# The first layer of a graph network moved into the cells of the later layers, edges sorted by pairs of node blocks, and the second layer set apart

## The chip, the cores and the metric

The kernel runs on one core of a Trainium2 chip. The metric is the device time of one execution in microseconds (us). Before the change it is 16670.39 us, the median of 10 runs that lie between 16644.18 and 16690.65.

A core has several engines that work side by side, each with a queue of its own in program order: PE (matrix multiplication), DVE (elementwise vector work), ACT (activations and copies), POOL (a second, slower vector engine, which here issues nearly all indirect transfers) and SP (which issues most plain transfers). Transfers run on 16 DMA engines. PE accumulates in PSUM, a memory of eight banks.

## The reference

A graph has N = 12500 nodes with 48 features and E = 400000 edges, sorted by their destination `dst`; `src` is random. Four graph layers follow each other, each with `x = layernorm(x + layer(x))`:

```python
# layer 0, edge attributes of width 32
h = relu(concat([x[dst], x[src], edge_attr_32]) @ W1 + b1)        # hidden 128
out = segment_sum(h @ W2 + b2, dst)
# layer 1: ci, cj from the degrees of src and dst
out = relu(where(in_deg > 0, segment_sum((x * ci)[src], dst) * cj, x) @ W.T + b)
# layer 2: row = src, col = dst
out = relu((segment_sum(norm * x[dst], src)) @ W.T + b)
# layer 3, edge attributes of width 40, per-edge gate
gate = silu(edge_attr_40 @ W1.T + b1) @ W2.T + b2 + sum(emb[z[src]] * (emb[z[dst]] @ adaptW.T))
msg = gate * x[dst] * (cutoff(distance) * node_mult[dst])
out = layernorm(x + segment_sum(msg, src) / clip(segment_sum(node_mult[dst], src)))
```

Layer 0 therefore needs, for each edge, a value of its source and of its destination, and sums by destination; layers 2 and 3 take from the destination and sum by source.

## The kernel before

Nodes lie in NB = 98 blocks of 128 and, two by two, in NP = 49 pairs. A *cell* is a pair of destination blocks (256 nodes) together with one source block (128 nodes); it has 128 slots for its edges. With one edge per lane, the cells of one destination pair make a matrix of 128 slots by 98 source blocks. Once an edge sits in a slot, its source features are picked out by a matrix multiplication with a one-hot matrix (its source block is known), and sums go through another one-hot matrix. No transfer per edge is needed then. All is in `by_cells` (line 55), and runs in stages that follow each other:

- **Histogram** (L291 to L311): the degree of every source. A hardware loop of 25 rounds takes 125 chunks of 128 edges each. For each chunk DVE makes two one-hot matrices, `c_ol` (L307) of the low seven bits and `c_oh` (L309) of the high bits, and PE multiplies them into PSUM.
- **Flat copies and tables** (L314 to L443): `dst`, `src` and the cutoff factor are turned by PE transposes and written flat to memory; `starts` holds where each block's edges begin. `qtab` holds, per source node, `x @ W1b` (128 values) and its embedding (32); `ptab` holds, per destination node, `x @ W1a + b1`, the adapted embedding and `node_mult` (161 values), split in three bfloat16 parts whose sum is the float32 value.
- **Layer 0** (L446 to L544): a hardware loop over the 98 destination blocks. A block's edges are read through a window of CW = 34 chunks of 128. DVE makes one one-hot matrix of the whole window, `c_wturned` (L482, 128 by 4352). For each chunk POOL gathers 128 rows of `qtab` with an indirect transfer (L260, called at L501), PE adds the edge attributes' part (L508) and the destination's part through the one-hot matrix and the three parts of `ptab` (L513), DVE adds the gathered rows (L529) and makes the products of the embeddings (L530), ACT applies relu (L532), and PE sums into the block by a float32 one-hot matrix `c_whot` (L522, L534). Per edge, the logit and `node_mult` go to `lmtab`.
- **Bias and layer norm** of layer 0, and the features of layer 1 in three parts.
- **Edges to cells, and layer 1** (L552 to L812), written out without a hardware loop. `to_cells` (L588) takes the 34 chunks of a block in steps of four: a one-hot matrix of the source block (L618), the gate's first layer on PE over the transposed attributes `c_sea` (L625), silu on ACT (L628), then per chunk PE's running counts `c_pp` (`tri`, L634), DVE's rank of the edge in its cell from them (L638), the gate's second layer on PE (L641), and `rest` (L642), which completes the counts and waits for the rank. ACT forms the record (L646). Every 12 chunks `scatter` (L657) works out where each edge goes, and POOL writes one record of 51 values per edge with an indirect transfer per chunk (L686). Layer 1 of an earlier pair (`layer1`, L735) is a Python generator; `advance` runs two of its steps after each four chunks, so its instructions stand between those of `to_cells` in the queues.
- **Middle of layer 1** (to L837): degree scaling, a 48 by 48 linear map, layer norm.
- **Layer 2** (L840 to L908): a hardware loop of 7 rounds of 14 source blocks; for each, the 49 pairs' features by one-hot matrices (`c_dhot` L869, L883), sums by `c_os` (L876).
- **Layer 3** (from L911): a hardware loop of 7 rounds of 7 pairs; per pair its records `c_rc` are read, features picked by `c_phot` (L962, L972), added up from three parts (L985), multiplied into the records (L988), and summed for each of the 98 source blocks by a float32 one-hot matrix (L980, L944) into the accumulator `c_acc` (L947).

`gather` (L259) and `one_hots` (L268, whose line stands for every caller in the profile: L270) are helpers. Within a stage, the order on each engine is settled by the compiler's scheduler from the written order and the buffers that come free. A flag, counted from broken assumptions (edges not sorted, a cell with over 128 edges, a window too small), chooses a slow general path at the end; on these inputs it isn't taken.

Of the kernel before, what the change touches and what calls it, by code (L numbers as in the profile page):

```python
# [54 lines left out]
def by_cells(ctx: ExitStack, tc: tile.TileContext, a: dict, out: bass.AP, flag):  # L55
# [17 lines left out]
    CW = -(-int(E / NB + 4.2 * (E / NB) ** 0.5) // P)  # L73
    W = CW * P
    UP = largest_divisor(NP, 7)
    UB = 2 * UP
# [4 lines left out]
    Q0 = HID + DG  # L81
    R = D + 3
    D3 = 3 * D
    CELLS = NB * SLOTS
    DUMP = NI * CELLS
    KP = -(-NB // 3)
    CP = 12
# [6 lines left out]
    src_f = dram.tile([E], I32, name="c_src_f")  # L94
    dst_f = dram.tile([E], I16, name="c_dst_f")
    cut_f = dram.tile([E], F32, name="c_cut_f")
    dst_rows = dram.tile([NCH, P], F32, name="c_dst_rows")
    first_f = dram.tile([P], I32, name="c_first_f")
    qtab = dram.tile([NB * P, Q0], F32, name="c_qtab")
    ptab = dram.tile([NB * P, 3 * T0], BF16, name="c_ptab")  # L100
    embtab = dram.tile([a["emb"].shape[0], 2 * DG], F32, name="c_embtab")
    lmtab = dram.tile([NB * P, 2 * CW], F32, name="c_lmtab")
    htab = dram.tile([NB * P, D], F32, name="c_htab")
    recs = [dram.tile([DUMP + 2 * NI * W, R], F32, name=f"c_rec{u}") for u in range(UP)]

    pair_d = dram.tile([NP, CELLS], BF16, name="c_pair_d")
    block_d = dram.tile([NB, NP * SLOTS], BF16, name="c_block_d")

# [11 lines left out]
    cols_f = const.tile([P, P], F32, name="c_cols_f")  # L120
    nc.vector.tensor_copy(cols_f, cols_i[:, :P])
    cols1_b = const.tile([P, 2 * P], BF16, name="c_cols1_b")
    nc.vector.tensor_scalar(cols1_b, cols_i, 1.0, None, op0=ALU.add)
    cols1_f = const.tile([P, P], F32, name="c_cols1_f")
    nc.vector.tensor_scalar(cols1_f, cols_i[:, :P], 1.0, None, op0=ALU.add)
# [9 lines left out]
    deg1 = const.tile([P, UB], F32, name="c_deg1")  # L135
# [5 lines left out]
    dump_i = const.tile([P, 2 * NI, CW], I32, name="c_dump_i")  # L141
    nc.gpsimd.iota(dump_i, pattern=[[W, 2 * NI], [1, CW]], base=DUMP, channel_multiplier=CW)
    dump_at = const.tile([P, 2 * NI, CW], F32, name="c_dump_at")
# [3 lines left out]
    block_i = const.tile([P, NB], I32, name="c_block_i")  # L147
    nc.gpsimd.iota(block_i, pattern=[[P, NB]], base=0, channel_multiplier=0)
    block_at = const.tile([P, NB], F32, name="c_block_at")
    nc.vector.tensor_copy(block_at, block_i)  # L150
# [28 lines left out]
    nc.sync.dma_start(w1c[0:DE, :], a["L0_W1"][2 * D : 2 * D + DE, :])  # L179
    w2 = load("w2", [HID, D], a["L0_W2"])  # L180
# [3 lines left out]
    g1T = load("g1T", [DR, D], a["L3_W1T"])  # L184
# [83 lines left out]
    def one_hots(o, codes, n, w):  # L268

        nc.vector.tensor_tensor(  # L270
            o[:, :n, :].rearrange("p j (a t) -> p j a t", t=2),
            cols1_b[:, :w].rearrange("p (o a t) -> p o a t", o=1, t=2).to_broadcast([P, n, w // 2, 2]),
            codes[:, :, None, :].to_broadcast([P, n, w // 2, 2]),
            op=ALU.is_equal,
        )

    def window_at(b):
        return nc.values_load(
            starts[0:1, ds(b, 1)] if not isinstance(b, int) else starts[0:1, b : b + 1],
            engines=(ET.SP,),  # L280
            min_val=0,
            max_val=E - W,
            skip_runtime_bounds_check_because="the smaller of two, and not negative",
        )

    def of_window(t, at):

        return t[ds(at, W)].rearrange("(p c) -> p c", c=CW)


    nc.vector.memset(degs["src"], 0.0)  # L291
    with tc.tile_pool(name="c_hk", bufs=2) as hk, tc.tile_pool(name="c_hoh", bufs=6) as hoh, tc.tile_pool(
        name="c_hps", bufs=1, space=PSUM
    ) as hps:
        with tc.For_i(0, NCH, CA) as i:
# [3 lines left out]
            for part, op, arg in (("hi", ALU.logical_shift_right, 7), ("lo", ALU.bitwise_and, 127)):  # L299
                v_i = hk.tile([P, CA], I32, name=f"c_{part}_i")  # L300
                nc.vector.tensor_scalar(v_i, ki, arg, None, op0=op)
                half[part] = hk.tile([P, CA], F32, name=f"c_{part}")
                nc.vector.tensor_copy(half[part], v_i)
            pd = hps.tile([P, NB], F32, name="c_pd")
            for c in range(CA):
                ol = hoh.tile([P, P], BF16, name="c_ol")
                nc.vector.tensor_scalar(ol, cols_b, half["lo"][:, c : c + 1], None, op0=ALU.is_equal)  # L307
                oh = hoh.tile([P, NB], BF16, name="c_oh")
                nc.vector.tensor_scalar(oh, cols_b[:, :NB], half["hi"][:, c : c + 1], None, op0=ALU.is_equal)  # L309
                nc.tensor.matmul(pd, ol, oh, start=(c == 0), stop=(c == CA - 1))  # L310
# [3 lines left out]
    with tc.tile_pool(name="c_fe", bufs=1) as fe, tc.tile_pool(name="c_few", bufs=3) as few, tc.tile_pool(  # L314
# [18 lines left out]
        for key in ("dst", "src", "cut"):  # L333
            kf = fold
            if key != "cut":
                ki = fe.tile([P, NCH], I32, name=f"c_fki_{key}")
                nc.sync.dma_start(ki, a[key + "T"])
                kf = fe.tile([P, NCH], F32, name=f"c_fkf_{key}")
                nc.vector.tensor_copy(kf, ki)
            for c in range(0, NCH, CT):  # L340
                pt = fep.tile([CT, P], F32, name="c_fpt")
                nc.tensor.transpose(pt, kf[:, c : c + CT], ident)
                flat, kind = {"src": (src_f, I32), "dst": (dst_f, I16), "cut": (cut_f, F32)}[key]
                t = few.tile([CT, P], kind, name=f"c_ft_{key}")
                (nc.vector.tensor_copy if key == "dst" else nc.scalar.copy)(t, pt)
                nc.sync.dma_start(flat.rearrange("(c p) -> c p", p=P)[c : c + CT, :], t)
                if key == "dst":
                    u = few.tile([CT, P], F32, name="c_ft_row")
                    nc.scalar.copy(u, pt)
                    nc.scalar.dma_start(dst_rows[c : c + CT, :], u)  # L350
# [17 lines left out]
        low = fe.tile([P, 1], F32, name="c_flow")  # L368
        nc.vector.tensor_scalar(low, first, float(E - W), None, op0=ALU.min)
# [183 lines left out]
    with tc.tile_pool(name="c_s1", bufs=1) as s1:  # L553
# [12 lines left out]
        with tc.tile_pool(name="c_s1r", bufs=2) as lr, tc.tile_pool(name="c_s1t", bufs=1) as lt, tc.tile_pool(  # L566
# [237 lines left out]
            for p in (NP - 2, NP - 1):  # L804
                if p < 0:
                    continue
# [881 lines left out]
```

## Time and profile before

The profiled execution's own time is 16669.57 us; its span from the first to the last instruction is 16667.8 us, so 1.8 us lie outside. The mean granted clock of PE is 0.739 of full speed. The page gives the busy shares of the span: PE 77%, PE's weight loads 60%, DVE 58%, POOL 42%, ACT 32%.

The stages can be told apart in the page's 40 slices and bounded in the timeline:

| stage | from to (us) | length (us) | per unit |
|---|---|---|---|
| histogram | 0 to 1104 | 1104 | 44.2 per round |
| copies and tables | 1104 to 1416 | 312 | |
| layer 0 | 1416 to 6135 | 4719 | 48.16 per block |
| bias, norm | 6135 to 6216 | 81 | |
| to cells, layer 1 | 6216 to 11844 | 5628 | 114.9 per pair |
| middle of layer 1 | 11844 to 12000 | 156 | |
| layer 2 | 12000 to 13188 | 1188 | 12.1 per block |
| its end | 13188 to 13344 | 156 | |
| layer 3 | 13344 to 16570 | 3226 | 65.8 per pair |
| end | 16570 to 16668 | 98 | |

How to read the views: *busy* is the time in which an engine had an instruction under way; instructions overlap on PE, so a mean duration there is longer than the distance from one start to the next. That distance, taken from the timeline, is what one instruction costs when many follow each other. The *granted clock* is a share of PE's full speed. A group of instructions has its line, engine, operation, output and inputs, count, busy time and mean, and then the idle time before them with what ended it.

### The profile page before, as it was taken

Reading aid. Unit: us, or ns where it says so; the run is one execution under the profiler, and the core shown is the slowest. Engines: PE = TensorE matmul, PEld = TensorE weight load, DVE = VectorE, ACT = ScalarE, POOL = GpSimd, SP = SyncE. Lnnn points to the kernel's source line nnn. Section 1 sums busy time; section 2 is a strip of 40 time slices with the busy share of each in tenths; the row PEclk is TensorE's granted clock in tenths of the full one; section 3 lists DMA queues with packets and bytes.
Section 4 is the critical chain, followed back from the end, with each engine's and each line's share of the span. In section 5 each row is a group of like instructions: output and inputs, shape, how many; then the busy total and the mean of one; then the engine's idle time right before and its main releaser. Section 6 shows DMA issues by size and latency. Waiting matters only on the chain. (4 is left out here: it accounts for less than half of the span.)

```text
span 16667.8 us, 263542 instructions
## 1 busy us (share of the span) xinstructions
PE 12760.9 (77%) x90916; PEld 9936.1 (60%) x90917; DVE 9585.4 (58%) x34506; ACT 5293.4 (32%) x11631; POOL 7078.5 (42%) x6776
## 2 busy tenths in 40 slices
PE   6655666666666559989988989988698788888886
PEld 2225555555555545555555555555587677777776
DVE  9974443443444443444444444444577688888888
ACT  0004444444444434444444444444366500000000
POOL 0006777777777755666566666666200000000000
PEclk9999888878878875666666666666699866666666
DMA  0025444444444432222222222222233222222222
GB/s 2 1 42 145 117 132 120 124 126 120 125 122 127 122 89 72 81 79 86 80 80 86 82 79 87 87 74 85 79 125 141 83 94 93 87 84 93 87 87 65
DMA packets 604921, 1537.81 MB, mean 92 GB/s; under 512 B 298614, under 2 KB 458790, under 8 KB 514518
## 3 DMA queue, kind: packets, MB, share of 16 engines
q1 hardware_dynamic: 280116, 1009.83, 18.9%
q0 software_dynamic: 269728, 363.67, 8.9%
q10 hardware_dynamic: 53778, 147.83, 2.3%
q8 instruction: 713, 11.68, 0.3%
q14 instruction: 586, 4.80, 0.1%
HBM read 1270.69 MB, written 250.08 MB: 91 GB/s over the span
## 5 line engine op out<-in xcount | busy, mean ns | idle before, releaser
L686 POOL DMA_INDIRECT c_rec<-c_srt,c_sat x3332 | 3393.6, 1018 | 2276.2 <-issue 1305.2
L260 POOL DMA_INDIRECT c_wq<-c_qtab,c_wix x3332 | 3581.9, 1075 | 1175.3 <-issue 953.4
L638 DVE CUSTOM_DVE_ANT_0 c_sjunk<-c_pp,c_soh 128x98 f32<-128x98 f32 x3332 | 857.3, 257 | 2255.6 <-PE c_pp L634 2246.9
L508 PE MATMUL c_wpl<-c_w1c,c_eat 128*128 128x128 f32 x6664 | 1177.3, 307 | 1176.6 <-ACT c_lm L531 971.2
L944 PE MATMUL c_pa<-c_rc,c_os 128*128 128x49 f32 x9604 | 1861.3, 347 | 252.1 <-DVE c_rc L988 251.5
L944 PEld LDWEIGHTS c_pa<-c_rc,c_os 128*128 128x128 f32 x9604 | 1718.1, 263 | 352.4 <-issue 167.3
L625 PE MATMUL c_sph<-c_sea,c_g1T 40*48 40x512 f32 (+1 forms) x1764 | 1778.4, 1097 | 21.5 <-ACT c_hid L628 21.5
L508 PEld LDWEIGHTS c_wpl<-c_w1c,c_eat 128*128 128x128 f32 x6664 | 979.2, 213 | 1200.1 <-ACT c_lm L531 989.8
L534 PE MATMUL c_wpa<-c_whot,c_wh 128*128 128x128 f32 x6664 | 1188.8, 329 | 638.8 <-ACT c_lm L531 606.4
L641 PE MATMUL c_spg<-c_g2x,c_hid 128*128 128x48 f32 x6664 | 1438.5, 372 | 141.0 <-ACT c_srt L646 137.8
L646 ACT ACTIVATE c_srt<-c_spg,c_slm,c_scut 128x48 f32<-128x48 f32 x3332 | 1064.0, 391 | 1495.9 <-PE c_spg L641 856.9
L534 PEld LDWEIGHTS c_wpa<-c_whot,c_wh 128*128 128x128 f32 x6664 | 1020.9, 232 | 782.1 <-ACT c_lm L531 734.9
L641 PEld LDWEIGHTS c_spg<-c_g2x,c_hid 128*128 128x128 f32 x6664 | 1344.8, 289 | 210.4 <-ACT c_srt L646 166.7
L972 PE MATMUL c_pm<-c_yp,c_phot 128*128 128x144 bf16 x9604 | 1167.0, 284 | 343.8 <-DVE c_phot L962 294.4
L642 PEld LDWEIGHTS <-c_rest 128*128 128x128 bf16 x3332 | 471.2, 142 | 1569.4 <-issue 1569.4
L743 PE MATMUL c_pa<-c_msg,c_od 128*128 128x144 bf16 x9604 | 1262.8, 279 | 174.4 <-ACT c_msg L764 168.2
L504 ACT COPY c_eat<-c_wea 32x384 f32<-32x384 f32 (+1 forms) x1176 | 1020.7, 870 | 876.4 <-PE c_wpl L508 715.1
L972 PEld LDWEIGHTS <-c_phot 128*128 128x128 bf16 x9604 | 997.9, 135 | 427.8 <-issue 177.5
L522 DVE TENSOR_TENSOR c_whot<-c_cols_f,c_wlo 128x384 f32<-128x384 f32 (+1 forms) x1176 | 625.7, 534 | 1011.2 <-PE c_wpa L534 1006.6
L980 DVE TENSOR_SCALAR c_os<-c_cols_f,c_rc 128x128 f32<-128x128 f32 x4802 | 1153.3, 277 | 61.2 <-DMA c_rc<-c_rec 61.2
L529 DVE TENSOR_TENSOR c_wh<-c_wq,c_wpl 128x384 f32<-128x384 f32 (+1 forms) x1176 | 622.1, 529 | 964.4 <-DMA c_wq<-c_qtab,c_wix 762.5
L226 ACT ACTIVATE c_ln_v<-c_ln_v,c_eps 128x98 f32<-128x98 f32 x5 | 1.9, 377 | 3407.7 <-DVE c_ln_v L225 3407.7
(248 smaller groups left out, 22769.5 us busy)
## 6 DMA issues: line engine op xcount, KB each, us to landing
c_rc<-c_rec SPq DMA_DIRECT2D x98, 2499.0 KB
c_drows<-c_block_d SPq DMA_DIRECT2D x98, 1568.0 KB
c_rec<-c_blank ACTq DMA_DIRECT2D x49, 2499.0 KB
c_drow<-c_dst_f SPq DMA_DIRECT2D x98, 1088.0 KB
c_srow<-c_row_s SPq DMA_DIRECT2D x98, 1056.0 KB
c_prows<-c_pair_d SPq DMA_DIRECT2D x98, 1056.0 KB
c_sea<-in_eaT_dram SPq DMA_DIRECT2D x98, 680.0 KB
c_wea<-in_eaT_dram SPq DMA_DIRECT2D x98, 544.0 KB
```

The source lines that it names most:

```text
L260: nc.gpsimd.indirect_dma_start(out=t, out_offset=None, in_=tab, in_offset=bass.IndirectOffsetOnAxis(ap=idx[:, c : c + 1], axis=0))
L504: nc.scalar.copy(eat[0:DE, :n, :], eac[:, c : c + n, :])
L508: nc.tensor.matmul(pl[:, j, :HID], eat[:, j, :], w1c, start=j == 0, stop=False, skip_group_check=True)
L534: nc.tensor.matmul(pa, h[:, j, :], o[:, j, :], start=c + j == 0, stop=c + j == CW - 1)
L625: nc.tensor.matmul(ph[:, :n, :], g1T, eac[:, c : c + n, :], start=True, stop=True)
L641: nc.tensor.matmul(pg[:, j, :], hid[:, j * P : (j + 1) * P], g2x, start=True, stop=True)
L646: nc.scalar.activation(rt[:, c - c0 + j, 0:D], pg[:, j, :], AF.Identity, bias=lm[:, 0, c + j : c + j + 1], scale=cut[:, c + j : c + j + 1],)
L686: s = nc.gpsimd.indirect_dma_start(out=recs[u], out_offset=bass.IndirectOffsetOnAxis(ap=at_i[:, c : c + 1], axis=0), in_=rt[:, c, :], in_o ...
L743: nc.tensor.matmul(pa[:, half, :], od[:, j, half * P : (half + 1) * P], msg[:, j, :], start=k0 + j == 0 and half == 0, stop=k0 + j == NB - ...
L944: nc.tensor.matmul(late_acc[0][:, k % KA, :], os_[j], rc[:, k, 0:W3], start=True, stop=True)
L972: nc.tensor.matmul(pm[:, j, :], ohs[half][:, k + j - k0, :], yp[:, half, :], start=half == 0, stop=half == 1,)
L980: nc.vector.tensor_scalar(o, cols1_f, rc[:, k + j, D + 1 : D + 2], None, op0=ALU.is_equal)
```

## The change

The change rearranges layers 0, 1 and 3, and leaves layer 2's arithmetic as it is.

- **Windows by pairs.** `pair_chunks` sizes a window for a pair of blocks, starting at a whole chunk: CW = 68 chunks for a pair (57 for the last). Where the two blocks meet inside a window is bounded too: chunks up to HI = 35 may have edges of the first block, chunks from LO = 29 on of the second; only between them both are multiplied. The window's checks are new accordingly. The flat copies of `src` and of the cutoff go; the inputs, already chunk by chunk, are read directly.
- **Histogram.** One-hot matrices of five chunks by one instruction each (`same`, the former `one_hots`), with the codes in bfloat16 and doubled, in place of two instructions per chunk.
- **`qtab`** is stored by lanes and split in three bfloat16 parts, as `ptab` is.
- **Layer 0 in cells.** `to_cells` now also computes, per chunk, the edge attributes' and the destination's part of the hidden layer (L599), in window order, and ACT copies it to a record of 212 values (161 of the former layer 0, 48 of the gate, and three codes). The one-hot matrix of destinations is made for 8 chunks and a block at a time (`c_sturned`, L563). POOL writes records of 212 values into one of six rings of cells (`rings`), whose cells are blanked once, ahead of the histogram. There is no gather from `qtab` any more.
- **`layer0`**, a generator as `layer1` was, takes two pairs at a time, in items of nine source blocks of one pair: it reads the records of the cells, turns the codes by a PE transpose and memory, makes the one-hot matrix of the sources (L757), picks `qtab`'s rows by three multiplications (L766), adds (L781), multiplies the embeddings (L782), applies relu, and sums over both blocks of the pair at once by a float32 one-hot matrix of 256 columns (L774, L728). It finishes the gate's record of 51 values and writes it to `recs` for layer 3, ordered by source block. `advance` runs 2.25 of its steps after each four chunks. Pairs 0 and 1 are thus taken once pair 2 is on its way.
- **Layer 1** becomes a stage of its own with a hardware loop over the pairs (7 rounds of 7); its arithmetic is as before.
- **Layer 3** loops over the 98 source blocks (7 rounds of 14). For a block the records of all 49 pairs are read, and their weighted features summed in PSUM over the pairs. The products are split in three bfloat16 parts by two ACT copies and two POOL subtractions, and multiplied by a bfloat16 one-hot matrix (in place of DVE's float32 one and of the accumulator in SBUF).

The core of the diff:

```diff
+    CW, LO, HI, _ = pair_chunks(2 * P)
+    CL, _, HL, least = pair_chunks(N - (NB - 2) * P)
+    CP = 8
+    RB = 6
+    R0 = T0 + D + 3
+    KQ = 9
+    rings = [dram.tile([CELLS + CW * P, R0], F32, name=f"c_ring{u}") for u in range(RB)]
+    for ring in rings:
+        nc.scalar.dma_start(
+            ring[:CELLS, :].rearrange("(p k) r -> p k r", p=SLOTS), blank[:, None, :].to_broadcast([P, NB, R0])
+        )
 # histogram
-            for c in range(CA):
-                nc.vector.tensor_scalar(ol, cols_b, half["lo"][:, c : c + 1], None, op0=ALU.is_equal)
-                nc.vector.tensor_scalar(oh, cols_b[:, :NB], half["hi"][:, c : c + 1], None, op0=ALU.is_equal)
+            for c in range(0, CA, 5):
+                for part, w in (("lo", P), ("hi", NB)):
+                    hot[part] = hoh.tile([P, 5, w], BF16, name=f"c_o{part}")
+                    same(hot[part], cols_b, half[part][:, c : c + n, :], n, w)
 # layer 0 as a stage of its own
-            with tc.For_i(0, NI, 1) as i:
-                for u in range(UB):
...
-                        for j in range(n):
-                            gather(q[:, j, :], qtab, ix, c + j)
 # to_cells
+                    for j in range(0, n, 2):
+                        pl = lp2.tile([P, 2, T0], F32, name="c_spl")
...
+                        nc.scalar.copy(rt[:, at : at + m2, 0:T0], pl[:, :m2, :])
-                        nc.scalar.activation(
-                            rt[:, c - c0 + j, 0:D], pg[:, j, :], AF.Identity, bias=..., scale=...)
+                    nc.scalar.copy(
+                        rt[:, c - c0 : c - c0 + n, T0 : T0 + D], pg[:, : n * D].rearrange("p (j d) -> p j d", d=D)
+                    )
 # layer0(pairs), called with two pairs
+                    for j0 in range(0, n, J3):
+                        pm = lp2.tile([P, J3, Q0], F32, name="c_pm")
+                        for j in range(m):
+                            for part in range(3):
+                                nc.tensor.matmul(pm[:, j, :], row[:, j0 + j, :], it["q3"][:, j0 + j, part, :], ...)
+                        od = lw.tile([P, J3, 2 * P], F32, name="c_od")
+                        nc.vector.tensor_tensor(od[:, :m, :], cols1_f..., cd..., op=ALU.is_equal)
+                        nc.vector.tensor_add(h[:, :m, :], pm[:, :m, :HID], rc[:, j0 : j0 + m, :HID])
+                        nc.vector.tensor_mul(prod..., pm[:, :m, HID:Q0], rc[:, j0 : j0 + m, HID : HID + DG])
+                        nc.scalar.activation(h[:, :m, :], h[:, :m, :], AF.Relu)
+                        if late:
+                            sums(*late)
+                        late = (it, j0, m, od, h)
+                        yield
 # order of the work
-                    for _ in edges:
-                        advance(2)
+                for step, _ in enumerate(to_cells(p, windows[p])):
...
+                    advance(2.25)
 # layer 3
+                            m = rc[:, q : q + n, 0:W3]
+                            nc.vector.tensor_mul(rc[:, q : q + n, 0:D], rc[:, q : q + n, 0:D], hh[:, :n, :])
+                            nc.scalar.copy(ms[:, :n, 0, :], m)
+                            nc.gpsimd.tensor_sub(m, m, ms[:, :n, 0, :])
...
+                            nc.scalar.copy(ms[:, :n, 1, :], m[:, :n, :])
+                            nc.gpsimd.tensor_sub(ms[:, :n, 2, :], m[:, :n, :], ms[:, :n, 1, :])
+                                nc.tensor.matmul(pa, os_[:, j, :], ms[:, j].rearrange("p k d -> p (k d)"), ...)
```

## The prediction

> **What bounds the kernel now.** I read the page's slices first, then bounded the stages in the timeline and asked for one window per stage (length; busy time and count of PE, PE's weight loads, DVE, ACT, POOL; granted clock; DMA share; GB/s).
>
> ```profile
> 0.00:1104.00 1104.00, 753.84 (x3124) 324.94 (x3126) 1014.57 (x6389) 0.00 (x0) 1.50 (x9) 1.00 0.01 2
> 1416.00:6135.00 4719.00, 2921.20 (x23520) 2714.86 (x23520) 1939.35 (x4023) 1973.21 (x3822) 3581.64 (x3332) 0.82 0.46 124
> 6216.00:11844.00 5628.00, 5025.66 (x29581) 3205.30 (x29580) 2534.49 (x12753) 2344.88 (x5929) 3393.59 (x3332) 0.63 0.26 81
> 12000.00:13188.00 1188.00, 1078.51 (x14406) 945.92 (x14406) 906.60 (x2152) 817.06 (x1667) 0.00 (x0) 0.96 0.36 132
> 13344.00:16570.00 3226.00, 2707.24 (x19208) 2522.93 (x19207) 2802.12 (x8856) 0.00 (x0) 0.00 (x0) 0.66 0.23 87
> ```
>
> No engine bounds the whole. The histogram is DVE's (92%), layer 0 POOL's, cells with layer 1 PE's (89%, at clock 0.63), layer 3 DVE's (87%). The groups say why, and POOL's timeline in layer 0 shows its rhythm:
>
> ```profile
> L307 DVE TENSOR_SCALAR c_ol<-c_cols_b,c_lo 128x128 bf16<-128x128 bf16 x3125 | 769.6, 247 | 0.0
> L260 POOL DMA_INDIRECT c_wq<-c_qtab,c_wix x3332 | 3581.9, 1075 | 1175.3 <-issue 953.4 <-DVE c_whot L522 131.9 <-DMA c_wq<-c_qtab,c_wix 67.8
> L625 PE MATMUL c_sph<-c_sea,c_g1T 40*48 40x512 f32 x1568 | 1665.0, 1151 | 21.5 <-ACT c_hid L628 21.5
> L642 PE MATMUL c_pp<-c_soh,c_rest 128*128 128x98 bf16 x3324 | 835.3, 251 | 156.0 <-DVE c_srank L638 140.2
> L980 DVE TENSOR_SCALAR c_os<-c_cols_f,c_rc 128x128 f32<-128x128 f32 x4802 | 1153.3, 277 | 61.2 <-DMA c_rc<-c_rec 61.2
> L985 DVE TENSOR_REDUCE c_hh<-c_pm 128x144 f32<-128x432 f32 x1568 | 936.4, 598 | 52.3 <-PE c_pm L972 52.3
> masks.py:199 POOL TENSOR_SCALAR_AFFINE_SELECT c_ident<-c_ident 128x128 f32<-128x128 f32 x1 | 0.3, 292 | 1102.9 <-DVE c_deg_src L311 1102.9
> ```
>
> ```profile
> 3011.57 0.94 POOL L260 DMA_INDIRECT c_wq<-c_qtab,c_wix  x1 [0.30 <-issue]
> 3012.82 4.61 POOL L260 DMA_INDIRECT c_wq<-c_qtab,c_wix  x1 [0.30 <-issue]
> 3017.73 0.95 POOL L260 DMA_INDIRECT c_wq<-c_qtab,c_wix  x1 [0.30 <-issue]
> ```
>
> A gather follows the last after 1.25 us; the long one lies beside DVE's 4.1 us `c_wturned`. So 34 gathers make the 48.2 us of a block. In the cells' stage, scatters keep the same 1.27 us, 86 of a pair's 115 us: POOL has room there.
>
> **Prices.** Start to start in the timeline, at full clock (half is twice that): bf16 matmul of 98, 144, 161 columns 43, 62, 72 ns; float32 issues as two instructions, of 128 or 48 columns 112 ns each. DVE: bf16 compare 0.471 us per 768, 0.269 per 384 (0.526 ns an element); float32 with two inputs 0.469 per 384 (1.03 ns beyond a fixed 0.07); rank 0.185; int16 compare 0.92 ns an element; three-part sum 0.52.
>
> **The change part by part**, against the profiled execution (16669.6, span 16667.8; 0.8 under the median).
>
> *Histogram.* Per round 25 groups of a 640- and a 490-element bf16 compare: 0.404 + 0.325 = 0.73 us, 18.2, plus the present 4.5 at a round's edge: 22.7 x 25 = 568. **-536.** The rings' blanking (6 x 10.6 MB) lies here, on ACT's queue, where the DMA share is 0.01; at the rate of layer 0 (124 GB/s by a share of 0.46, so 270) it takes 235 us. Without that cover, up to +235.
>
> *Copies.* The turns of `src` and the cutoff took about 65 us; splitting `qtab` adds about 10: **-55.**
>
> *Layer 0 and cells (now 4719 + 5628 = 10347).* Per pair and 68 chunks:
> - PE: attributes 136 x 0.112 = 15.2; destination 225 x 0.072 = 16.2 (only about 7 chunks meet both blocks); gate one 34 instructions of 512, gate two 136 x 0.112 = 15.2; `tri`, `rest` 136 x 0.043 = 5.8; `qtab` 294 x 0.071 = 20.9; sums 196 of 256 columns; small ones 1.5. The wide float32 ones aren't in the trace as such: 512 columns take 0.957 now, read at a stride of 34 elements. Unstrided I scale the 0.112 for 128 columns, 0.448 and 0.224 (15.2 and 43.9); from above, 0.957 for 512 and its half, 32.5 and 94. I take the scaled one, since the rows without a stride are nearer. Sum **134** at full clock.
> - DVE: `c_od` 33 x 0.86 = 28.5; hidden adds 15.5; rank 12.6; `c_sturned` 10.5 x 1.1 = 11.6; gate's record 14.3; source one-hots 8.2; logits and products 9.6; `c_srow` 4.7; scatter's arithmetic, codes and heads 9.6: **115.** ACT about 50.
> - POOL: 68 x 1.27 = 86, some 100 with blocking. The 3332 gathers go.
> - DMA: ring read 10.6 MB, scatter 7.4, `qtab` 6, `c_srow` 3.2, others 7.3: 34.5 MB. At layer 0's 270 GB/s 128 us; at layer 3's 87/0.23 = 378, 91.
>
> So PE leads, and its clock matters. It is granted as 1.0 or 0.5 in windows of 3.4 us, and goes with the columns streamed per us (float32 twice per instruction): layer 2 1745 at 0.96, layer 0 1064 at 0.82, cells 901 at 0.63, layer 3 720 at 0.66. A pair here streams 280k. At clock 0.82 it would take about 195 us, 1430 per us, above layer 0's; that lifts the clock, so it settles near 0.95: 134/0.95 = 141. Of their length, cells and layer 2 spend 0.83 and 0.84 in matmuls by these prices; with 0.83, **170 us a pair.** ("TensorE: Matmul & The Clock Gate", Part 1, lets the clock follow how busy PE has been; here PE is 89% busy at 0.63 and 91% at 0.96, so by that rule alone the new stage could as well get 0.63, and it would be rival 1's sum.)
>
> The first 2.25 pairs have no layer 0 beside them, about 95 each (86 for POOL): 214. Then 46.75 x 170 = 7948. At the end the last pairs' layer 0, some 90 steps of 2.4: 217. Together 8379. Waits added: `rest` still waits for the rank, now behind a longer DVE queue with 0.86 us compares; 0.3 us more on each of 68 chunks would be 20 us a pair. Other work stands between `tri` and `rest`, and now PE idles 156/3324 = 47 ns there, so I count it within the 0.83. A record tile waits for the scatter of three pieces earlier, 60 us old; SP issues some 70 transfers a pair at 0.36 us, 25 us, and loads three items (22 us) ahead.
>
> *Layer 1 alone.* Per pair PE 294 x 62 ns = 18.2, DVE 19.8, ACT 13.5. Layer 2's rows, of the same kind, give 0.82 of the length to the busiest: 24 x 49 = 1176, plus 7 edges of 12: **+1260.** Its cover in the cells' stage is what it loses. The three together: 8379 + 1260 - 10347 = **-708.**
>
> *Bias, norm* **+17** (a load, an add); *layer 2* **+5** (codes loaded).
>
> *Layer 3.* Now 65.8 us for a pair, DVE 56.6. After, per block: `c_phot` 3.5, `c_os` as bf16 4.4 (17 x 0.26) where float32 cost 49 x 0.205 = 10, three-part sums 8.5, products 3.6, rest 0.5: DVE 20.5, in place of 28.3. PE 9.1, ACT 9.5. POOL 34 subtractions of 147 elements: no such row. From below, the select of 128 elements, 0.29; from above, a scatter's 1.27. The select is nearer; with a gap as between gathers (0.30) about 0.5: 17, and blocked by `c_phot` as the gather above was, 20.5. With 0.8: 25.6 x 98 = 2509, edges 7 x 14: 2607, **-619.** With 0.29 DVE leads: 24 x 98 + 98 = 2450 (-776). With 1.27 POOL takes 43 + 3.5: 4660, +1430.
>
> A rule speaks against this: "SBUF — State Buffer", section "SBUF: two separate sides", says VectorE in a two-port mode, or with two SBUF inputs against a GpSimd instruction that reads SBUF, and GpSimd shut each other out for a whole instruction. The 4.61 us gather agrees for the first. If it holds for `c_os` and the products too, POOL's 17 and DVE's 11.5 follow each other: 28.5 a block, 2890.
>
> Sum: -536 - 55 - 708 + 17 + 5 - 619 = -1896: **14,774.**
>
> **Rivals.**
> 1. *Slower: the clock stays low.* At 0.63 and 0.83 a pair takes 134/0.63/0.83 = 256: +46.75 x 86 = 18,800. It decides at 210.6 us a pair (1896/46.75 = 40.6 more), clock 0.77. For it: cells have the same mixture of short waits, and 0.63. Against: nearly twice the columns per us. Chance 0.08.
> 2. *POOL or the transfers bind more than forecast.* POOL at 30 us a block in layer 3: +430. Or rank waits and a DMA share of 0.75 hold a pair at 195: +1170. So 15,200 to 15,950. For it: DMA share never passed 0.46 before. Chance 0.27.
> 3. *PE fully fed.* 150 us a pair, PE's 141 over 0.94; layer 3 at 24: 14,774 - 935 - 157 = 13,680. For it: three independent streams of work. Against: no stage shows 0.94. Chance 0.10.
> 4. *Fallback or no change* can't be: the gathers are gone and each stage is rewritten. Chance of within 0.2%, about what measurement can tell: 0.01.
>
> The forecast has 0.54 (162 to 180 us a pair: 14,400 to 15,250 with layer 3's spread).
>
> **Range and chances.** 13,750 to 16,150: below it lies most of rival 3, above it rival 1. Faster 0.90: the forecast, rivals 2 and 3, less 0.01 for a rival 2 worse than priced; slower 0.09.
>
> **What would show it.** Right: histogram near 570; no gather on `c_qtab`; PE's clock above 0.9 from about 1,050 on, a pair every 170 us; DVE's idle time in layer 3 ended by PE and POOL busy under 20 us a block. Wrong: clock under 0.8 in the main stage; `rest` idle by more than 0.2 us each behind the rank; layer 3's sums waiting on POOL's subtractions, at over 0.6 us each.

## The result, and the profile after

The changed kernel takes 17376.86 us (median of 8 runs, 17340.5 to 17394.25) where the kernel before takes 16678.13: a ratio of 1.0416, 95% interval 1.0406 to 1.0425. It is slower by 4%; the prediction had 14,774, in a range of 13,750 to 16,150.

For two runs below, `blank3` and `all3`, the kernel before took 19,133 us in the same series; both were taken again in a series in which it took 16,663, and what slowed the first is open, since the record names its chip, 11, for a series with 16,693 too.

The stages of the profiled execution of 17336.35 us, beside the forecast's (us; "outside" is the 2 us around the span):

| stage | forecast | measured | difference |
|---|---|---|---|
| histogram, copies and tables | 825 | 1140 | +315 |
| edges to cells with layer 0 | 8379 | 10470 | +2091 |
| bias, norm, layer 1 | 1358 | 1303 | -55 |
| middle of layer 1 | 156 | 157 | +1 |
| layer 2 and its end | 1349 | 1323 | -26 |
| layer 3 | 2607 | 2854 | +247 |
| end and outside | 100 | 89 | -11 |

The miss is one large term and two small ones. The windows of those three, without the first 65 us (length; busy time and count of PE, PE's weight loads, DVE, ACT, POOL; granted clock; DMA share; GB/s):

```profile
65.00:639.00 574.00, 347.88 (x3060) 273.88 (x3058) 474.82 (x1357) 0.00 (x0) 0.19 (x1) 1.00 0.03 7
639.00:1140.00 501.00, 111.64 (x468) 98.46 (x468) 146.74 (x218) 123.90 (x140) 118.67 (x99) 1.00 0.77 192
```

```profile
1140.00:11610.00 10470.00, 7957.23 (x57303) 6297.77 (x57301) 5984.35 (x22799) 2484.49 (x5500) 3530.65 (x3321) 0.85 0.61 165
14393.00:17247.00 2854.00, 1621.15 (x14349) 1366.11 (x14346) 2599.14 (x5471) 964.51 (x3322) 1680.91 (x3323) 0.69 0.29 98
```

In the edges' stage nobody is full: PE 76%, DVE 57%, POOL 34%, DMA 61%. A stage of 10.5 ms with no full engine is a stage that waits. The groups of the page say for whom: after the second bar stands the idle time ahead of the group, and behind each arrow what ended most of it.

```profile
L622 PE MATMUL c_pp<-c_soh,c_rest 128*128 128x98 bf16 x3321 | 754.4, 227 | 2437.4 <-DVE c_srank L615 2431.3
L574 DVE COPY c_srt<-c_stail 128x24 f32<-128x24 f32 (+1 forms) x440 | 77.9, 177 | 2378.0 <-DMA c_ring<-c_srt,c_sat 2286.5
```

PE idles 2437 us ahead of `rest`, because the rank is late; and DVE, which makes the rank, idles almost the same 2378 us ahead of an instruction that costs 0.18 us: the copy of three codes per edge into a record tile (L574). What ends that wait is the landing of a scatter. The timeline of DVE, POOL and PE shows one such stretch:

```profile
6019.90 0.25 DVE L615 CUSTOM_DVE_ANT_0 c_sjunk<-c_pp,c_soh 128x98 f32<-128x98 f32 x1
...
6020.33 0.40 DVE L800 COPY c_g<-c_ccd 128x18 f32<-128x18 f32 x1
6030.05 0.17 DVE L574 COPY c_srt<-c_stail 128x12 f32<-128x12 f32 x1 [9.32 <-DMA c_ring<-c_srt,c_sat]
...
6035.55 0.25 DVE L615 CUSTOM_DVE_ANT_0 c_sjunk<-c_pp,c_soh 128x98 f32<-128x98 f32 x1
...
6042.98 0.15 DVE L637 TENSOR_SCALAR_CACHE_REDUCE c_sover<-c_srank 128x8 f32<-128x8 f32 x1
...
6045.17 0.16 DVE L650 TENSOR_TENSOR c_sat<-c_spos,c_dump_at 128x8 int32<-128x8 f32 x1
```

```profile
6017.21 0.96 POOL L652 DMA_INDIRECT c_ring<-c_srt,c_sat  x1 [18.72 <-ACT c_srt L603]
...
6026.15 0.97 POOL L652 DMA_INDIRECT c_ring<-c_srt,c_sat  x1 [0.30 <-issue]
6046.08 0.96 POOL L652 DMA_INDIRECT c_ring<-c_srt,c_sat  x1 [18.95 <-ACT c_srt L603]
```

```profile
6035.86 0.24 PE L622 MATMUL c_pp<-c_soh,c_rest 128*128 128x98 bf16 x1 [9.61 <-DVE c_srank L615]
```

A *piece* is eight chunks whose records share one record tile (`c_srt`) and are scattered together. L615 makes a chunk's rank, L637 to L650 the places of a piece.

DVE stops at 6020.7, with four of a piece's eight ranks made, and goes on at 6030.05, 3 us after POOL was done issuing the last of eight scatters (6026.15 + 0.97). From 2000 to 11000 us 343 of 380 such copies wait over 1 us, and these start 3.5 us (median) after the end of the latest scatter's issue. So the copy doesn't wait for an old scatter, but for the newest.

The order in DVE's queue shows why. Copies and ranks can be counted in the trace: with A the piece whose ranks are half made at 6020, the copy at 6030.05 is that of C, two pieces later. The queue holds four ranks of A, the copy for C, A's other four ranks (6035.55 to 6041.95), A's places (6042.98 to 6045.17), after which POOL may scatter A (6046.08), and then the first rank of the next piece (6047.22). In the written order the copy stands at the start of its own piece; in the queue 403 of 440 copies stand two pieces ahead, with one to seven of A's ranks behind them.

The codes are known early, so nothing but the tile holds the copy back, and the scheduler has moved it up to about where that tile can come free: with three tiles, C takes the tile of the piece just before A, whose scatter has only been issued. Behind the waiting copy stand A's remaining ranks; behind these A's places and scatter; and behind that scatter, by the same rule, the next copy. Scatter, landing, ranks, scatter: one loop, of 25 us for a piece and 214 us for a pair. That this loop sets the time is so far read from one trace; the next runs test it.

### The profile page after: what moved, and what is told of

It reads as the page before. It is cut to its first block, busy times and chain, and to the rows that moved or that the text cites. A ratio compares the mean times of both kernels' runs of the same rounds, so it can differ in the third digit from the quotient of the medians.

```text
span 17334.6 us, 299320 instructions
## 1 busy us (share of the span) xinstructions
PE 12319.0 (71%) x104699; PEld 10042.2 (58%) x104700; DVE 11421.7 (66%) x34047; ACT 5270.5 (30%) x12322; POOL 5336.6 (31%) x6764
## 5 line engine op out<-in xcount | busy, mean ns | idle before, releaser
L652 POOL DMA_INDIRECT c_ring<-c_srt,c_sat x3321 | 3530.6, 1063 | 6734.9 <-ACT c_h L785 3571.9
L728 PE MATMUL c_pa<-c_od,c_h 128*128 128x256 f32 x9604 | 3022.5, 446 | 8.0 <-ACT c_h L785 7.9
L728 PEld LDWEIGHTS c_pa<-c_od,c_h 128*128 128x128 f32 x9604 | 1895.6, 221 | 389.9 <-issue 193.2
L615 DVE CUSTOM_DVE_ANT_0 c_sjunk<-c_pp,c_soh 128x98 f32<-128x98 f32 x3321 | 853.1, 257 | 1261.3 <-PE c_pp L613 1251.3
L574 DVE COPY c_srt<-c_stail 128x24 f32<-128x24 f32 (+1 forms) x440 | 77.9, 177 | 2378.0 <-DMA c_ring<-c_srt,c_sat 2286.5
L774 DVE TENSOR_TENSOR c_od<-c_cols_f,c_ccd 128x768 f32<-128x768 f32 (+1 forms) x1617 | 1513.3, 943 | 188.9 <-PE c_pa L728 174.6
L766 PE MATMUL c_pm<-c_q,c_srow 128*128 128x160 bf16 x14406 | 1596.1, 248 | 27.3 <-DVE c_srow L757 14.7
L273 DVE TENSOR_TENSOR c_os<-c_cols_b,c_cs 128x384 bf16<-128x384 bf16 (+1 forms) x3332 | 1253.7, 394 | 243.5 <-PE c_pa L1014 211.7
L1108 PE MATMUL c_pm<-c_y,c_phot 128*128 128x144 bf16 x9604 | 1146.0, 282 | 324.6 <-DVE c_phot L1082 320.5
L766 PEld LDWEIGHTS <-c_srow 128*128 128x128 bf16 x14406 | 1204.8, 108 | 137.3 <-DVE c_srow L757 36.0
L599 PE MATMUL c_spl<-c_spb,c_sturned 128*128 128x161 bf16 x11010 | 1169.8, 241 | 0.0
L599 PE MATMUL c_spl<-c_w1c,c_feat 128*128 128x128 f32 x6642 | 1154.9, 294 | 1.2 <-DMA c_feat<-in_eaT_dram 1.2
```

Source lines behind the costliest of these rows:

```text
L273: nc.vector.tensor_tensor(o[:, :n, :].rearrange("p j (a t) -> p j a t", t=2), numbers[:, :w].rearrange("p (o a t) -> p o a t", o=1, t=2).t ...
L599: nc.tensor.matmul(to, lhs, rhs, start=k == 0, stop=k == len(todo) - 1, skip_group_check=True)
L615: nc.vector.tensor_tensor_reduce(junk, pp, oh[:, j, :], 1.0, 0.0, ALU.mult, ALU.add, accum_out=rank[:, c - c0 + j : c - c0 + j + 1],)
L652: s = nc.gpsimd.indirect_dma_start(out=rings[p % RB], out_offset=bass.IndirectOffsetOnAxis(ap=at_i[:, c : c + 1], axis=0), in_=rt[:, c, :] ...
L728: nc.tensor.matmul(pa[:, it["h"], :], h[:, j, :], od[:, j, :], start=k == 0 and it["h"] == 0, stop=k == NB - 1, skip_group_check=True,)
L766: nc.tensor.matmul(pm[:, j, :], row[:, j0 + j, :], it["q3"][:, j0 + j, part, :], start=part == 0, stop=part == 2,)
```

## The experiments

**1. Is it the number of record tiles, or the copy's place?** Three runs. The first takes six tiles:

```diff
-                        rt = lc.tile([P, CP, R0], F32, name="c_srt", bufs=3)
+                        rt = lc.tile([P, CP, R0], F32, name="c_srt", bufs=6)
```

> The changed kernel with six record tiles in place of three. In its trace DVE idles 2378 us at the copy of the codes into a record tile (L574), ended by the scatter's transfer, and PE idles 2437 us ahead of `rest`, behind the rank. Theory A, too few tiles: with six, the tile's scatter is five pieces old when the copy comes, the idle time goes, a pair takes 165 to 185 us in place of 213, the whole 15,400 to 16,400. Theory B, the copy's place in DVE's queue: the scheduler puts the copy as early as the tile can come free, with six tiles five pieces ahead of its use in place of two, so it meets a scatter just issued all the same: 17,100 to 17,500, and idle time at L574 above 1,500 us. Theory C, the long compares ahead of the rank hold PE, and the wait at L574 is only where the slack shows: 17,200 to 17,500 too, but with the idle time at L574 gone.

The second keeps three, but makes the codes depend on the ranks, so they can't stand ahead of them:

```diff
-                        nc.vector.tensor_copy(rt[:, :m, T0 + D : R0], tail[:, c : c + m, :])
...
                     if c + n == c0 + m:
+                        for k in range(3):
+                            nc.vector.scalar_tensor_tensor(
+                                rt[:, :m, T0 + D + k], rank[:, :m], 0.0, tail[:, c0 : c0 + m, k], op0=ALU.mult, op1=ALU.add
+                            )
                         scatter(p, c0, m, rank, off, kx, rt)
```

> The changed kernel with three record tiles, but the three code columns are written by instructions that read the piece's ranks, so they can't stand ahead of them in DVE's queue. Theory A, too few tiles: the same wait moves to ACT's copies into the record tile, 17,000 to 17,500. Theory B, place in the queue: DVE no longer idles ahead of the ranks of an older piece, a pair falls from 213 to 165 to 185 us, the whole to 15,300 to 16,300. Theory C, the long compares: 17,100 to 17,500.

The third does both:

> Both: codes written after the ranks, and six record tiles. Theory A alone: as with six tiles alone, 15,400 to 16,400. Theory B alone: as with the late codes alone, within 100 us. If both have a part, this is below either by more than 150 us.

Measured: six tiles 16785.78 us (ratio to the kernel before 1.0054, 1.0037 to 1.0071); late codes 15315.66 (0.9177, 0.9161 to 0.9192); both 15299.08 (0.9167, 0.9152 to 0.9183). A pair takes 202, 171 and 171 us. The page's groups of the kernel with six tiles:

```profile
L622 PE MATMUL c_pp<-c_soh,c_rest 128*128 128x98 bf16 x3321 | 739.1, 223 | 1973.6 <-DVE c_srank L615 1966.3
L574 DVE COPY c_srt<-c_stail 128x24 f32<-128x24 f32 (+1 forms) x440 | 79.5, 181 | 1685.0 <-DMA c_ring<-c_srt,c_sat 1603.5
```

and of the kernel with late codes and three tiles, with a window inside its edges' stage:

```profile
L621 PE MATMUL c_pp<-c_soh,c_rest 128*128 128x98 bf16 x3321 | 716.9, 216 | 810.7 <-DVE c_srank L614 798.4
```

```profile
2000.00:9000.00 7000.00, 6251.10 (x48140) 4971.15 (x48138) 5037.57 (x19902) 2108.79 (x4623) 3094.08 (x2799) 0.93 0.78 207
```

With twice the tiles most copies (305 of 440) stand five pieces ahead in place of two, and they still wait 1685 us. With the copy behind its ranks, three tiles are enough: PE is 89% busy at clock 0.93, and the wait for the scatter is gone (1.2 us in all at the new instructions). Six tiles on top of that change nothing. So it was the place in the queue (theory B); more tiles are not needed (A), and the long compares (C) do not hold PE once the copy is out of their way. That six tiles alone still brought 590 us, which B alone did not expect, says that the number has a part as long as the copy stands early; why it is that much was not tried.

**2. Who leads a pair once that wait is gone?** Late codes, and the sums over a block in bfloat16:

```diff
-                        od = lw.tile([P, J3, 2 * P], F32, name="c_od")
+                        od = lw.tile([P, J3, 2 * P], BF16, name="c_od")
...
-                        late = (it, j0, m, od, h)
+                        hb = lw.tile([P, J3, HID], BF16, name="c_hb")
+                        nc.scalar.activation(hb[:, :m, :], h[:, :m, :], AF.Relu)
...
+                        late = (it, j0, m, od, hb)
```

> Late codes, and layer 0's one-hot matrix and hidden layer in bfloat16 for the sums over a block, which gives up precision: PE's share of the prices falls from 134 us a pair to about 101 (196 x 0.224 to 98 x 0.108), DVE's from 115 to 102. If PE leads a pair, as forecast: 101/0.95/0.83 = 128 us a pair in place of 171, the whole about 13,300. If the chain of counts, rank and `rest`, or another order of the queues, leads: 155 to 171 us a pair, 14,600 to 15,300.

Measured 13827.38 us (0.8287, 0.8273 to 0.8301), 139 us a pair in place of 171: between "PE leads" (128) and "a chain leads" (155 to 171), and nearer to the first. A window inside the edges' stage of this run, beside the same stretch of the run with late codes alone (the second line):

```profile
2000.00:7500.00 5500.00, 4787.56 (x42350) 3713.62 (x42347) 4299.83 (x19534) 1924.11 (x4433) 2745.19 (x2678) 0.94 0.95 253
2000.00:7500.00 5500.00, 4903.51 (x37750) 3899.29 (x37748) 3952.65 (x15613) 1653.15 (x3623) 2417.35 (x2193) 0.93 0.78 207
```

For a pair, PE's busy time falls by 31 us (152 to 121), as much as the pair does, and DVE's by 14. So it fits that PE leads a pair of 171 us, though the run alone doesn't show it, since it shortened DVE's compares too. At 139 us the transfers are nearly full, with a DMA share of 0.95, which may be what keeps the pair from 128; that was not tried.

**3. Layer 3: what holds it at 1.41 us a group?** Its groups in the changed kernel, over a window inside the stage; the duration stands after the busy time:

```profile
L1118 DVE TENSOR_REDUCE c_hh<-c_pm 128x144 f32<-128x432 f32 x1372 | 816.6, 596 | 19.6 <-PE c_pm L1108 19.4
L1122 DVE TENSOR_TENSOR c_rc<-c_rc,c_hh 128x144 f32<-128x144 f32 x1372 | 692.4, 510 | 0.0
L273 DVE TENSOR_TENSOR c_os<-c_cols_b,c_cs 128x384 bf16<-128x384 bf16 x1373 | 604.8, 446 | 25.8 <-PE c_pa L1093 25.6
```

The sum that reads PSUM takes its 0.596 us as before the change (0.598). The product takes 0.510 where it took 0.299, the compare 0.446 where layer 2's takes 0.354: both read two inputs from SBUF while POOL subtracts. Three runs test it. With the subtractions on DVE:

```diff
-                            nc.gpsimd.tensor_sub(m, m, ms[:, :n, 0, :])
+                            nc.vector.tensor_sub(m, m, ms[:, :n, 0, :])
```

and the same for the second one;

> The changed kernel with layer 3's two subtractions per group on DVE in place of POOL. In its trace a group of three pairs takes DVE 1.41 us, with `c_os` at 0.45 us and the product at 0.51, where they took 0.35 and 0.30 without POOL beside them. Theory P, POOL and DVE shut each other out in these two: on DVE the subtractions add 2 x 0.22 us, the others fall back to 0.27 and 0.22 from start to start, 1.45 us a group: layer 3 within 150 us of 2854, the whole 17,250 to 17,550. Theory Q, POOL takes work off DVE and the longer durations have another cause: DVE takes 1.41 + 0.44 = 1.85 us a group, +0.44 x 17 x 98 = +730, the whole about 18,100.

with the three-part sums in PSUM (`hh` from a PSUM pool of three banks, nothing else changed):

> The changed kernel with layer 3's three-part sums `c_hh` written to PSUM, so that the product after them has one input in SBUF and one in PSUM; the subtractions stay on POOL. If POOL and DVE shut each other out only where DVE reads two inputs from SBUF, the product falls from 0.51 us to about 0.3 and a group from 1.41 us to about 1.2: layer 3 -300 to -400, the whole 16,950 to 17,100. If POOL holds DVE up whatever DVE reads, or DVE is slow for its own reasons: 17,300 to 17,450.

and in float32, without any split:

```diff
-                            os_ = lw.tile([P, J3, P], BF16, name="c_os3")
-                            same(os_, cols1_b, cs[:, q : q + n, :], n, P)
+                            os_ = lw.tile([P, J3, P], F32, name="c_os3")
+                            nc.vector.tensor_tensor(os_[:, :n, :], cols1_f..., cs..., op=ALU.is_equal)
...
-                                nc.tensor.matmul(pa, os_[:, j, :], ms[:, j].rearrange("p k d -> p (k d)"), ...)
+                                nc.tensor.matmul(pa, os_[:, j, :], m[:, j, :], start=q + j == 0, stop=q + j == NP - 1)
```

> The changed kernel with layer 3 in float32: no split, no ACT copies, no POOL subtractions, a float32 one-hot matrix and float32 sums; blocks and order stay. DVE by its prices alone 0.47 + 0.52 + 0.22 = 1.21 us a group in place of 1.41, without POOL beside it. If POOL's company is what cost layer 3 its time: about 24.6 us a block, 2510 in place of 2854, the whole about 17,040. If PE at half clock then leads (6 x 0.12 + 6 x 0.21 = 2.0 us a group): up to 3500, the whole up to 18,000.

Measured: 17492.64 us (1.0482, 1.0464 to 1.0499), 17371.32 (1.0421, 1.0398 to 1.0445) and 17186.92 (1.0304, 1.0280 to 1.0329). Their edges' stages are some 80 us longer than in the first profile, as is that of the changed kernel run once more; so the stages are compared: layer 3 takes 2854 us in the changed kernel, 2898 with the subtractions on DVE, 2778 with sums in PSUM, 2602 in float32. The groups with the subtractions on DVE:

```profile
L273 DVE TENSOR_TENSOR c_os<-c_cols_b,c_cs 128x384 bf16<-128x384 bf16 x1349 | 465.5, 350 | 0.2
L1089 DVE TENSOR_TENSOR c_ms<-c_rc,c_ms 128x147 bf16<-128x147 f32 x1350 | 412.8, 306 | 1.6 <-ACT c_ms L1088 1.6
L1125 DVE TENSOR_TENSOR c_rc<-c_rc,c_ms 128x147 f32<-128x147 f32 x1350 | 407.5, 307 | 11.7 <-ACT c_ms L1124 2.9
L1122 DVE TENSOR_TENSOR c_rc<-c_rc,c_hh 128x144 f32<-128x144 f32 x1350 | 398.8, 301 | 0.0
```

With POOL silent, compare and product are back at 0.350 and 0.301, and two more instructions of 0.31 fit into nearly the same time: POOL's help was worth 44 us of 2854. The changed kernel's own trace agrees: from 14,700 to 17,200 us the 250 products with no subtraction beside them took 0.299 us each, the 1206 beside one 0.551. The Trainium skill's rule in "SBUF — State Buffer", section "SBUF: two separate sides", is that a DVE instruction with two SBUF inputs and a GpSimd instruction that reads SBUF shut each other out. These rows fit it. The forecast's sum by that rule, 2890, lies within 36 us of the 2854 measured, but this is partly luck: the sum left out that POOL waits for ACT's copies, 0.75 us a group in that window. In the run with PSUM the product falls to 0.297, and beside a subtraction it is no longer (0.291), as the rule has it; but the time hardly moves, because POOL's own chain is next. The product and POOL's timeline there:

```profile
L1124 DVE TENSOR_TENSOR c_rc<-c_rc,c_hh 128x144 f32<-128x144 f32 x1408 | 411.3, 297 | 0.0
```

```profile
15804.82 0.47 POOL L1091 TENSOR_TENSOR c_ms<-c_rc,c_ms 128x147 bf16<-128x147 f32 x1 [0.43 <-ACT c_ms L1090]
15805.24 0.43 POOL L1127 TENSOR_TENSOR c_rc<-c_rc,c_ms 128x147 f32<-128x147 f32 x1
15806.11 0.47 POOL L1091 TENSOR_TENSOR c_ms<-c_rc,c_ms 128x147 bf16<-128x147 f32 x1 [0.43 <-ACT c_ms L1090]
```

Subtract, wait 0.43 us for ACT's copy, subtract: 1.29 us a group. The expectation of 1.2 had left that chain out. Float32 drops POOL and ACT alike, and gains 252 us.

**4. The blanking of the rings.** ACT's queue in the changed kernel, after the histogram:

```profile
642.32 185.01 ACTq L293 DMA_DIRECT2D c_ring<-c_blank  x5
827.37 40.23 ACTq L331 DMA_DIRECT2D c_dist<-in_ewT_dram  x1
```

One ring was blanked ahead of the histogram's loop, and held up its first load (the first DVE work of the loop starts at 53.7 us); the other five were issued after the loop, for 185 us, ahead of the load of the distances. Moved into the loop's rounds:

```diff
-    for ring in rings:
-        nc.scalar.dma_start(ring[:CELLS, :]..., blank[:, None, :].to_broadcast([P, NB, R0]))
...
         with tc.For_i(0, NCH, CA) as i:
+            for ring in rings:
+                nc.scalar.dma_start(
+                    ring[ds(i * 5, 5 * CA), :].rearrange("(p k) r -> p k r", k=5),
+                    blank[:CA, None, :].to_broadcast([CA, 5, R0]),
+                )
```

> The changed kernel with the rings blanked in the rounds of the histogram's loop, 625 rows of each ring a round, in place of six transfers ahead of it. In the changed kernel's trace one ring is blanked ahead of the loop, which starts its first DVE work at 54 us, and five after it, with ACT's queue busy on them from 642 to 827 us ahead of the load of the distances. If the blanking is the whole of the first 1140 us' excess (forecast 825): 200 to 300 us less, 17,080 to 17,180. If the copies and tables are longer for another reason, or a loop that waits for its transfers grows as much as it saves: 17,300 to 17,420.

Measured 17517.62 us (1.0512, 1.0487 to 1.0536): no gain. The copies and tables did shrink, from 501 to 300 us, but a round grew from 23 to 36 us. The next round's load is issued only after the transfers (their packets end at 115.3 us, the load is issued at 117.2), and DVE waits for it:

```profile
102.86 0.26 DVE L323 TENSOR_TENSOR c_deg_src<-c_deg_src,c_pd 128x98 f32<-128x98 f32 x1 [0.66 <-PE c_pd L320]
119.09 0.23 DVE L309 TENSOR_SCALAR c_hi_i<-c_ki 128x125 int32<-128x125 int32 x1 [15.97 <-DMA c_ki<-in_srcT_dram]
```

Longer rows, issued once the codes of the round have landed:

```diff
+                nc.scalar.dma_start(ring[ds(i * 5, 5 * CA), :].rearrange("(p k) r -> p (k r)", k=5), zero[:CA, :])
```

> The changed kernel with the rings blanked in the histogram's rounds, but in transfers of 4240 bytes a row in place of 848, from a tile that ACT makes once the round's codes have landed. In the run with rows of 848 bytes a round grew from 23 to 35 us, and the copies and tables after it shrank from 501 to 300. If it was the many short rows: a round back to 23 to 26 us, the whole 200 to 300 below the run of the changed kernel in this call. If transfers of a loop's round can't be hidden in it: a round above 30 us, and no more than 100 us saved.

Measured 17525.74 us (1.0504, 1.0486 to 1.0521), a round 37 us: not the rows. The trace's packets show what was: 5.5 and 4.6 of the blanking's packets were under way at a time, at 97 and 104 GB/s, where the ring ahead of the loop in the changed kernel had 17 under way at 240 GB/s. The difference left is 125 lanes against 128. With 128 (`ds(i * 5, 5 * P)`, `zero`):

> As the blanking in long rows, but each transfer from 128 lanes (640 rows of a ring, 15 of them again in the next round) in place of 125. In the run before, 4 to 5 transfers were under way at a time at 100 to 130 GB/s; ahead of the loop in the changed kernel, from 128 lanes, 17 at 260 GB/s. If the 125 lanes were the cause: 3.26 MB in 13 us, hidden under a round's 18 us, a round back to 23 to 25 us, the whole 17,130 to 17,250. If a loop's round can't hide transfers at all: 17,500 to 17,540 again.

> The long rows from 128 lanes on another chip too. If the last call's chip left it undisturbed, as its stages suggest: 17,100 to 17,250, some 250 us below the changed kernel.

Measured 17161.43 us the first time and 17182.65 (1.0312, 1.0289 to 1.0336) the second: a round of 23.4 us, 15 packets under way at 390 GB/s, and the edges begin 268 us earlier than in the changed kernel run again. DVE now waits little for the next round's load:

```profile
105.14 0.23 DVE L304 TENSOR_SCALAR c_hi_i<-c_ki 128x125 int32<-128x125 int32 x1 [3.35 <-DMA c_ki<-in_srcT_dram]
```

The changed kernel run again:

> The changed kernel once more, on the chip of this call: the edges' stage of the other runs without the late codes lies 70 to 90 us above that of the first profile. If that is the chip or the run: 17,380 to 17,480 here.

which took 17434.62 us (1.0446, 1.0428 to 1.0463). So a loop's round can hide transfers; those from 125 lanes were slow for their number of lanes, the only thing that changed between the last two edits. Other numbers of lanes were not tried.

**5. Together.** Late codes, layer 3 in float32, and the blanking in each of its three forms:

> Codes written after the ranks (15,316 alone), blanking in the loop, layer 3 in float32. If the three parts add up: 15,316 less what the other two runs of this call save; by their expectations 14,700 to 14,800. If one hides behind another, more by over 100 us.

> Late codes, layer 3 in float32, and the blanking in long rows in the loop. Late codes with layer 3 in float32 and the blanking in short rows took 15,107. If the long rows hide: 14,700 to 14,850. If not: 15,000 to 15,120.

> Late codes, layer 3 in float32, and this blanking. If it hides: 14,750 to 14,900, the lowest of the kernels that keep float32's precision. If not: 15,100 to 15,150.

> The same kernel on another chip: on the last call's chip the kernel before took 19,133 us in place of 16,680, and in the edges' stage PE, DVE and ACT show idle time ended by nothing of this program. If that was the chip: 14,750 to 14,900 here, and the edges' stage at 171 us a pair. If the combination itself is slow: 16,000 again.

Measured 15106.77 us (0.9064, 0.9044 to 0.9085), 15138.71 (0.9073, 0.9055 to 0.9090), 16027.33, and, the same kernel again, 14784.71 (0.8869, 0.8849 to 0.8890). The last is the fastest version that keeps float32's precision. Its parts add up: 15,316 - 268 - 252 = 14,796. Its edges' stage took 195 us a pair the first time and 171 the second, with nothing changed in the program, so the combination itself isn't slow. The window of its histogram:

```profile
0.00:600.00 600.00, 355.44 (x3125) 279.81 (x3126) 490.99 (x1433) 63.10 (x52) 1.67 (x12) 1.00 0.36 142
```

The blanking is now the DMA share of 0.36 under the histogram (0.03 in the changed kernel).

## Why the prediction was wrong

- **The step that failed** is one clause: "A record tile waits for the scatter of three pieces earlier, 60 us old", costed at nothing. It took the written order for the order in the queue. The copy stands two pieces ahead of its use and its scatter is 3.5 us old; DVE idles 2378 us ahead of it, and PE 2437 us behind it. With the copy put behind its ranks a pair takes 171 us where 170 were forecast; the stage comes to 8406 us by the starts of layer 1 in the two traces, where 8379 were forecast. The prediction named the sign to look for (`rest` idle by over 0.2 us each behind the rank; it was 0.73), but put it down to long compares, which the runs rule out as its main cause: without the early copy 0.24 us of it is left.
- **The prices held.** In the trace with late codes, float32 matmuls of 256 columns start 0.216 us apart (0.224 estimated), of 512 unstrided 0.467 (0.448). The clock is 0.93 (0.95), and with the forecast's 134 us of matmuls that makes 0.84 of a pair's length (0.83). That PE leads a pair fits the run with bfloat16 sums, which doesn't show it alone. Rival 1, a clock that stays at 0.63, did not come: it was 0.85 even with the waits.
- **Rival 2** came in kind, by 247 us in layer 3. The forecast took blocking of POOL by `c_phot` alone, and nothing for DVE: its terms make (4.4 + 8.5 + 3.6)/17 = 0.97 us of DVE for a group, and the trace has 1.41, with POOL and DVE in each other's way. The rule set against it, two SBUF inputs, was the better guide.
- **The blanking** was counted as covered by the histogram, with up to +235 if not. The cover was there, the order was not: five of six transfers stood after the loop in ACT's queue. It cost 268 us by the run that hides it, of the 315 us that the first stages were longer; the other 47 were not followed up.
- **Histogram, layer 1, layer 2** were right: a round of 23.0 us against 22.7, layer 1 with its norm 1303 against 1358.
- **The chances** went wrong with that clause: the rival for slower was priced by the clock, and rival 2 let rank waits hold a pair at 195 us, not at 214. What stands in the queue behind a waiting instruction was asked of `rest`, and not of a copy that costs 0.18 us.

The profile before held a small sign of it. There the same copy (L616) had six record tiles, of 51 values an edge, and the change left three, of 212. Even with six, DVE idled 85 us ahead of the copy for a block's last piece, half of it ended by a scatter:

```profile
L616 DVE COPY c_srt<-c_stail 128x30 f32<-128x30 f32 x97 | 20.6, 212 | 85.4 <-DMA c_rec<-c_srt,c_sat 46.2 <-issue 34.6
```

## What to carry to other kernels

An instruction whose inputs are early and whose output tile is late can be moved up in its queue to about where the tile comes free, and then everything behind it waits for whatever frees the tile. Here more tiles mostly moved it further up and took away under a third of the wait, while tying it to a late input put it where it belongs. So when a change lets an instruction write to a tile that a transfer empties, read the order in which that queue ran, not the written one. When a stage has no full engine, follow the idle time from the busiest engine one step back, and then one further: here from PE to the rank, and from DVE to a copy.

## What was not expected of the hardware

- POOL's two subtractions of a group were worth 44 us of 2854 to DVE, whose own instructions read two SBUF inputs: product 0.299 to 0.510 us, compare 0.354 to 0.446.
- A transfer from SBUF of 125 lanes kept about 5 packets under way at some 100 GB/s, whether in rows of 848 or 4240 bytes; in rows of 4240 bytes one of 128 lanes kept 15 at 390 GB/s, and a round that moves as much fell from 37 to 23.4 us by that change alone.
